# Filling work dealt out anew around the last routing, and expert weights fetched in two halves, in an attention and mixture-of-experts layer

## The chip, the cores and the metric

The kernel runs on one core of one Trainium2 chip. The metric is the device time in microseconds of one execution, as the median of several runs. All arithmetic is in 32-bit floats. The engines are called TensorE (PE), VectorE (DVE), ScalarE (ACT), GpSimd (POOL) and SyncE (SP). SP computes nothing: it reads numbers into registers, waits on semaphores and issues DMA transfers, in the order of its own instruction stream.

## The reference

The input is 8 sequences of 512 tokens with 512 features. The layer is attention followed by a mixture of experts, each with a layer norm before it, a layer norm behind it and a residual:

```
x = x + layernorm(attention(layernorm(x)))      # 16 heads, latent keys and queries, softmax
x = x + layernorm(moe(layernorm(x)))

moe(t) = routed(t) + shared(t)
shared(t) = relu(t @ shared_up)**2 @ shared_down           # 512 -> 1024 -> 512
scores = sigmoid(t @ router.T)                             # 16 experts, in 4 groups
chosen = the best 2 experts within the best 2 groups       # ranked by scores + e_bias
w = scores[chosen] / sum(scores[chosen])
routed(t) = sum over e in chosen of  w[e] * relu(t @ w_up[e])**2 @ w_down[e]    # 512 -> 256 -> 512
```

## The kernel before, in words

**Stages.** The attention stage works through the 8 sequences, each in 16 steps (4 groups of 4 heads, by 4 tiles of 128 queries). A step issues the score matmuls, softmax, transposes and weighted sums of its own. Work of the sequence before (output projection, norms, routing) and of the next one (projections) is put at fixed steps by `beside`. Every routed token row is scattered by GpSimd into a table in DRAM, sorted by expert (`send`, L780). When the last sequence is routed, `plan` counts the tiles of each expert and makes `lists`: for each place a first row in the table, an expert, and a flag that says whether the expert differs from that of the place three before. Then comes the routed stage over 79 tiles of 128 gathered rows, and then a tail, in which the shared expert of the last three half sequences is computed and all results are summed, normed and stored.

**The order of PE.** PE's instructions run in the order in which the program traces them. The other engines are ordered by a scheduler; in the routed stage and in the tail, SP's order is the program's too.

**Filling work.** The shared expert is computed in half sequences, numbered k = 0 to 15. Each consists of eight up chunks (L817; cost 1.72 in the planner's unit, microseconds: 8 matmuls as the trace counts them, a relu on ScalarE at L825, a square at L827 on VectorE or at L829 on ScalarE) and four down pieces (L836, cost 3.43). The halves 0 to 12 wait in the list `waiting`, and `fill(room)` takes pieces from its front while room is left. In the last sequence (`last_sequence`), fills stand between the output projection, the transposes of the normed rows, the router's logits and `assign`. `assign` turns the chosen experts into table rows through two small matmuls (ps_pos, L755 and L756), and `plan` needs one more (ps_plan, L908). What is left in `waiting` is emptied after the plan by `fill(1e9)`. The squares of halves 13 to 15 (`LATE = 3`) are on ScalarE, the others on VectorE.

**The routed stage.** There are three sets of weight tiles (`NBUF = 3`; `set_up` and `set_down`, 512 KB each), and places that are neighbours in time use different sets. In turn n, PE transposes the rows of place n+1 (pt_g, L966; the copy is at L968), computes the up product of place n (hg, L983) and the down product of place n-1 (yg, L998). VectorE scales the result, and GpSimd adds it into a sum in DRAM by scattered rows (L1007). SP fetches ahead, at the end of the turn:

```
            if n + AHEAD < NTILES:
                fetch_rows(places[n + AHEAD])          # AHEAD = 3
            if n + NBUF - 1 < NTILES:
                fetch_weights(places[n + NBUF - 1])    # place n + 2
```

`fetch_rows` reads one list entry into a register (L948) and issues one transfer (L950). `fetch_weights` reads two entries, the expert and the flag (L953, L954), and issues two conditional transfers, up (L956) and down (L959); where the flag is 0, nothing is moved. The weights of place n+2 go into the set that place n-1 has used, so the up transfer waits until `up(n-1)` is done and the down transfer until `down(n-1)` is done. The weight tiles also take memory that the tiles of the attention stage held, so that the first fetch waits for the scatters out of `ao`.

Of the kernel before, what the change touches and what calls it, by code (L numbers as in the profile page):

```python
# [18 lines left out]
P = 128  # L19
# [20 lines left out]
def sandwich_kernel(  # L40
# [28 lines left out]
    nc = tc.nc  # L69

    B, S, D = x.shape
# [26 lines left out]
    NTILES = (TOP_K * T) // P + NE - 1  # L98
    NBUF = 3
    THIRD = -(-NTILES // NBUF)  # L100
    NPLACES = NBUF * THIRD
    places = [j for j in range(NPLACES) if j % NBUF * THIRD + j // NBUF < NTILES]
# [157 lines left out]
    def normalize(dst, src, rstd, off, i):  # L260
        nc.scalar.activation(
            dst, src, AF.Identity, bias=off[:, i : i + 1], scale=rstd[:, i : i + 1]
        )
# [310 lines left out]
    def last_sequence(prev, fill):  # L574


        b = B - 1
        xT[b] = sh.tile([P, NK, S], F32, tag="xnT", name=f"xT_{b}")
        pt_den = ps_o.tile([P, NT, P], F32, tag="o", name=f"pt_d_{b}_last")
        ps_ctx = ps_o.tile([P, S], F32, tag="o", name=f"o_{b}_last")  # L580
        acc = [None] * NT

        def most(i):
            acc[i] = ps_o.tile([P, D], F32, tag="o", name=f"ps_acc_{i}")
            nc.tensor.matmul(acc[i], lhsT=ones[0:1, :], rhs=bo[0:1, :], start=True, stop=False)
            for c in range(NK - 1):
                out_of_group(acc[i], b, c, i)

        denominators(b, NGRP - 1)
        for i in range(2):  # L590
            most(i)
        keys_first(*prev, range(4))
        turn_denominators(b, NGRP - 1, pt_den)
        weighted_sum(b, NGRP - 1, ps_ctx)
        for i in range(NT):
            if i > 1:
                most(i)
            out_of_group(acc[i], b, NK - 1, i)
        fetch_x()
        for i in range(NT):  # L600
            ps, row, xb = acc[i], ao[:, i, 0:D], res[b][:, i, :]
            normalize(row, ps, *norm_stats([ps], f"o{b}_{i}"), 0)
            nc.vector.tensor_tensor(xb, xb, row, ALU.add)
            normalize(row, xb, *norm_stats([xb], f"f{b}_{i}"), 0)
        fill(3.4)
        for i in range(NT):
            turn_rows(ao, xT[b], i, f"f{b}")
            if i > 0:
                logits(b, i - 1)
            if i < NT - 1:  # L610
                fill(1.7)
        logits(b, NT - 1)
        sigmoid(b)
        groups(b)
        experts(b)
        fill(5.1)
        assign(b)
        weights(b)
        for i in range(NT):
            send(b, i)  # L620
# [190 lines left out]
    def shared_up_chunk(b, a, i):  # L811

        if i == 0:
            hT[b] = sh.tile([P, NH, HALF], F32, tag="hT", name=f"hT_{b}_{a}")
        ps = ps_o.tile([P, S], F32, tag="o", name=f"h_{b}_{a}_{i}")
        for k in range(NK):
            nc.tensor.matmul(  # L817
                ps[:, 0:HALF],
                lhsT=wsu[:, k, i * P : (i + 1) * P],
                rhs=xT[b][:, k, a * HALF : (a + 1) * HALF],  # L820
                start=(k == 0),
                stop=(k == NK - 1),
            )
        h = hT[b][:, i, :]
        nc.scalar.activation(h, ps[:, 0:HALF], AF.Relu)  # L825
        if 2 * b + a < 2 * B - LATE:
            nc.vector.tensor_tensor(h, h, h, ALU.mult)  # L827
        else:
            nc.scalar.square(h, h)  # L829
# [107 lines left out]
    def routed(rt, lists, expert):  # L937

        xg, xgT, hg, share, to = {}, {}, {}, {}, {}
        sets = []  # L940
        for i in range(NBUF):
            sets.append((
                rt.tile([P, NK, INTER], F32, name=f"set_up_{i}"),
                rt.tile([P, NI, D], F32, name=f"set_down_{i}"),
            ))

        def fetch_rows(j):
            row = nc.sync.value_load(lists[0:1, 0, j : j + 1], min_val=0, max_val=NE * REGION)  # L948
            xg[j] = rt.tile([P, W], F32, tag="xg", name=f"xg_{j}", bufs=4)
            nc.sync.dma_start(xg[j], table[bass.ds(row, P), :])  # L950

        def fetch_weights(j):
            e = nc.sync.value_load(lists[0:1, 1, j : j + 1], min_val=0, max_val=NE - 1)  # L953
            load = nc.sync.value_load(lists[0:1, 2, j : j + 1], min_val=0, max_val=1)  # L954
            wu, wd = sets[j % NBUF]
            nc.sync.dma_start(  # L956
                wu, w_up[bass.ds(e, 1)].rearrange("o (c p) i -> p (o c) i", p=P), cond=load
            )
            nc.sync.dma_start(  # L959
                wd, w_down[bass.ds(e, 1)].rearrange("o (c p) d -> p (o c) d", p=P), cond=load  # L960
            )

        def turn(j):
            pt = ps_o.tile([P, NK, P], F32, tag="o", name=f"pt_g_{j}")
            for k in range(NK):
                nc.tensor.transpose(pt[:, k, :], xg[j][:, k * P : (k + 1) * P], ident)  # L966
            xgT[j] = rt.tile([P, NK, P], F32, tag="xgT", name=f"xgT_{j}", bufs=4)
            nc.scalar.copy(xgT[j], pt)  # L968

            each = rt.tile([P, NE], F32, tag="each", name=f"each_{j}", bufs=2)  # L970
            share[j] = rt.tile([P, 1], F32, tag="share", name=f"share_{j}", bufs=4)
            nc.vector.scalar_tensor_tensor(
                each, experts_, expert[:, j : j + 1], xg[j][:, D:NUMBER],
                ALU.is_equal, ALU.mult, accum_out=share[j],
            )
            to[j] = rt.tile([P, 1], I32, tag="to", name=f"to_{j}", bufs=6)
            nc.vector.tensor_copy(to[j], xg[j][:, NUMBER : NUMBER + 1])

        def up(j):
            ph = ps_o.tile([P, S], F32, tag="o", name=f"hg_{j}")  # L980
            for i in range(NI):
                for k in range(NK):
                    nc.tensor.matmul(  # L983
                        ph[:, i * P : (i + 1) * P],
                        lhsT=sets[j % NBUF][0][:, k, i * P : (i + 1) * P],
                        rhs=xgT[j][:, k, :],
                        start=(k == 0),
                        stop=(k == NK - 1),
                    )
            h = rt.tile([P, NI * P], F32, tag="hgT", name=f"hgT_{j}", bufs=4)  # L990
            nc.scalar.activation(h, ph[:, 0 : NI * P], AF.Relu)  # L991
            nc.vector.tensor_tensor(h, h, h, ALU.mult)  # L992
            hg[j] = h

        def down(j, n):
            py = ps_o.tile([P, D], F32, tag="o", name=f"yg_{j}")
            for i in range(NI):
                nc.tensor.matmul(  # L998
                    py,
                    lhsT=hg[j][:, i * P : (i + 1) * P],  # L1000
                    rhs=sets[j % NBUF][1][:, i, :],
                    start=(i == 0),
                    stop=(i == NI - 1),
                )
            y = rt.tile([P, D], F32, tag="y", name=f"y_{j}", bufs=4)
            nc.vector.tensor_scalar(y, py, share[j], None, ALU.mult)  # L1006
            nc.gpsimd.indirect_dma_start(  # L1007
                out=sums[n % 2][:, :],
                out_offset=bass.IndirectOffsetOnAxis(ap=to[j], axis=0),
                in_=y,  # L1010
                in_offset=None,
                compute_op=ALU.add,
            )

        AHEAD = 3
        for n in range(NBUF - 1):
            fetch_weights(places[n])
        for n in range(AHEAD):
            fetch_rows(places[n])
        turn(places[0])  # L1020
        for n in range(NTILES + 1):
            if n + 1 < NTILES:
                turn(places[n + 1])
            if n < NTILES:
                up(places[n])
            if n > 0:
                down(places[n - 1], n - 1)
            if n + AHEAD < NTILES:
                fetch_rows(places[n + AHEAD])
            if n + NBUF - 1 < NTILES:  # L1030
                fetch_weights(places[n + NBUF - 1])

# [53 lines left out]
    LATE = 3  # L1088
# [65 lines left out]
    with tc.manual_schedule(engines={mybir.EngineType.PE}):  # L1154
# [8 lines left out]
        def fill(room):  # L1163
            while waiting and room > 0:
                cost, f, _ = waiting.pop(0)
                f()
                room -= cost
# [47 lines left out]
        while waiting[0][0] == UP:  # L1215
            waiting.pop(0)[1]()
        last_sequence(prev, fill)
        lists, expert = plan()
        fill(1e9)
    until_routed.close()  # L1220
# [3 lines left out]
    for k in range(2 * B - LATE, 2 * B):  # L1224
# [4 lines left out]
        for n, (cost, f) in enumerate(shared_list(k, one)):  # L1229
            items.append((f, 2 * k if n == NH + 3 else None))  # L1230
            if len(items) > 6 and n % 2 == 1:
                c = next(early, None)
# [12 lines left out]
    with tc.manual_schedule(engines={mybir.EngineType.PE, mybir.EngineType.SP}):  # L1245
        n = 0
# [48 lines left out]
```

## Time and profile before

| | |
|---|---|
| three runs | 1643.39 us median, 1639.08 to 1643.61 |
| profiled execution | 1646.31 us, of which the span of instructions is 1644.6 us |
| PE busy | 1563.2 us (95% of the span) |
| VectorE, ScalarE, GpSimd busy | 1003.3, 843.5 and 208.0 us |
| mean granted clock of PE | 0.975 |
| routed stage | first rows turned at 1225.8 us, last scatter issued at 1550.4 us |

The profile is of one execution on the chip. Times in it are microseconds from the first instruction. PE is the matmul stream and PEld the loads of stationary operands beside it. PEclk is the share of full speed at which PE's clock was granted. A row of a timeline gives start, duration, engine, line, operation, `out<-in`, the number of instructions that are merged in it, and in brackets the idle time before it and what ended it. A row of a line's instructions gives the count, then the shortest, median and longest duration in ns, then the first and last start. A row of SP's waits gives who waited for whom, the microseconds in total, the times and the longest. SP's instructions are not counted as busy time on the page. A row by windows gives the busy time of PE, PEld, DVE, ACT and POOL with the number of instructions, then PE's clock, the mean busy share of the 16 DMA engines and the GB/s that they moved.

### The profile page before, as it was taken

The page shows a single profiled execution, that of the slowest core. Times are in us where ns is not written, and L with a number is a line of the kernel's source. Part 1 is how long each engine was busy: PE and PEld are TensorE (multiplying, and loading weights), DVE is VectorE, ACT ScalarE, POOL GpSimd, SP SyncE. Part 2 cuts the span into 40 slices and gives each one's busy share as a digit, 9 for nine tenths or more (in the row PEclk, how much of TensorE's full clock was granted, in tenths as well). Part 3 has the DMA queues.
Part 4 walks back from the last instruction along what each step waited for, and adds up shares of the span by engine and source line. Part 5 has one row for each costly group of instructions (what it writes and reads, how often), then busy time and mean ns, then how long its engine had stood idle before and what let it go on. Part 6 is the DMA issues. An engine that isn't in the chain of part 4 may idle for free.

```text
span 1644.6 us, 25313 instructions
## 1 busy us (share of the span) xinstructions
PE 1563.2 (95%) x8010; PEld 916.2 (56%) x8010; DVE 1003.3 (61%) x2942; ACT 843.5 (51%) x1998; POOL 208.0 (13%) x193
## 2 busy tenths in 40 slices
PE   6999799999999999999999999999989999899996
PEld 3554454555455545555544545456557777677754
DVE  4667874776587577758766866774433333333298
ACT  5876665575466557556655755654312222122245
POOL 0000011002000100200010020011014333333300
PEclk8999899999999999999999999999989999999998
DMA  4016666567566655755564565552457778997695
GB/s 130 1 36 198 186 201 199 145 192 246 158 182 187 214 165 167 219 154 153 154 200 125 150 210 149 166 149 87 165 178 133 141 138 191 310 244 154 134 366 200
DMA packets 170022, 282.89 MB, mean 172 GB/s; under 512 B 21152, under 2 KB 86688, under 8 KB 169632
## 3 DMA queue, kind: packets, MB, share of 16 engines
q1 hardware_dynamic: 153392, 242.72, 48.2%
q0 software_dynamic: 16496, 38.54, 11.8%
q8 instruction: 64, 1.05, 0.3%
q14 instruction: 70, 0.57, 0.1%
HBM read 224.43 MB, written 132.92 MB: 217 GB/s over the span
## 4 chain that ended last, share of the span: by engine, by line
PE 67%; DVE 15%; DMA 7%; ACT 7%; SPq 2%; issue 2%; DVEq 0%; POOL 0%; POOLq 0%; ACTq 0%
PE y L836 9%; PE hg L983 7%; PE yg L998 7%; PE h L817 6%; PE pt L454 6%; PE ps_ao L623 6%; PE s L387 5%; PE o L521 4%; DMA set_up<-in_L_ffn_w_up_dram 2%; DMA turned<-pB 2%; DVE pB L473 2%; ACT pb L417 2%; PE ps_v L347 2%; PE pt_g L966 2%; PE ps_k L360 1%
## 5 line engine op out<-in xcount | busy, mean ns | idle before, releaser
L417 ACT ACTIVATE pb<-pb,nmax 128x512 f32<-128x512 f32 x256 | 182.7, 715 | 191.1 <-DVE nmax L405 184.1
L817 PE MATMUL h<-xT,wsu 128*128 128x256 f32 x1024 | 240.7, 391 | 0.6 <-ACT hT L825 0.6
L836 PE MATMUL y<-wsd,hT 128*128 128x512 f32 x512 | 231.6, 603 | 0.0
L405 DVE CUSTOM_DVE_ANT_0 pb<-s,rope 128x512 f32<-128x512 f32 x256 | 166.7, 685 | 97.5 <-PE s L387 97.0
L817 PEld LDWEIGHTS h<-xT,wsu 128*128 128x128 f32 x1024 | 198.1, 196 | 48.8 <-issue 10.2
L417 ACT ACTIVATE p<-p,nmax 128x512 f32<-128x512 f32 x256 | 181.5, 710 | 29.9 <-DVE nmax L405 29.5
L405 DVE CUSTOM_DVE_ANT_0 p<-s,rope 128x512 f32<-128x512 f32 x256 | 167.6, 684 | 27.1 <-PE s L387 26.4
L454 PEld LDWEIGHTS pt<-ident,p 128*128 128x128 f32 x1024 | 111.6, 142 | 99.7 <-issue 22.7
L473 DVE STREAM_TRANSPOSE pB<-pb 128x1024 f32<-128x1024 f32 x108 | 133.8, 1238 | 49.8 <-DMA turned<-pB 36.7
L983 PE MATMUL hg<-xgT,set_up 128*128 128x128 f32 x1264 | 155.1, 276 | 8.2 <-DMA set_up<-in_L_ffn_w_up_dram 7.1
L836 PEld LDWEIGHTS y<-wsd,hT 128*128 128x128 f32 x512 | 97.0, 193 | 116.2 <-issue 108.6
L387 PE MATMUL s<-k,q 32*128 32x512 f32 x1024 | 156.7, 647 | 0.0
L454 PE MATMUL pt<-ident,p 128*128 128x128 f32 x1024 | 142.2, 281 | 12.7 <-DVE ctx L528 12.6
L983 PEld LDWEIGHTS hg<-xgT,set_up 128*128 128x128 f32 x1264 | 147.4, 192 | 11.4 <-issue 5.8
L1007 POOL DMA_INDIRECT sums<-y,to x79 | 122.6, 1552 | 222.4 <-DVE y L1006 190.1
L998 PE MATMUL yg<-set_down,hgT 128*128 128x512 f32 x316 | 148.5, 593 | 0.0
L495 POOL COPY wide<-rden 128x512 f32<-128x512 f32 x32 | 19.6, 613 | 977.3 <-PE ps_ao L623 233.7
L992 DVE TENSOR_TENSOR hgT<-hgT 128x256 f32<-128x256 f32 x79 | 33.6, 426 | 156.4 <-ACT hgT L991 156.4
L521 PE MATMUL o<-pTb,v 128*32 128x512 f32 x496 | 114.5, 604 | 7.8 <-DMA pTb<-turned 7.8
L968 ACT COPY xgT<-pt_g 128x512 f32<-128x512 f32 x79 | 46.2, 586 | 139.4 <-PE pt_g L966 139.4
L521 PE MATMUL o<-pT,v 128*32 128x512 f32 x496 | 116.5, 604 | 0.2 <-DVE pT L464 0.2
L623 PE MATMUL ps_ao<-wo,ctx 128*128 128x512 f32 x224 | 98.5, 593 | 0.0
(233 smaller groups left out, 2073.2 us busy)
## 6 DMA issues: line engine op xcount, KB each, us to landing
turned<-pB SPq DMA_DIRECT2D x432, 128.0 KB
pTb<-turned SPq DMA_DIRECT2D x108, 512.0 KB
set_up<-in_L_ffn_w_up_dram SPq DMA_DIRECT2D x79, 512.0 KB
set_down<-in_L_ffn_w_down_dram SPq DMA_DIRECT2D x79, 512.0 KB
xg<-table SPq DMA_DIRECT2D x79, 272.0 KB
end<-sums SPq DMA_DIRECT2D x32, 512.0 KB
sums<-table SPq DMA_DIRECT2D x40, 256.0 KB
x<-in_L_attn_x_dram SPq DMA_DIRECT2D x32, 256.0 KB
```

Source lines behind the costliest of these rows:

```text
L387: nc.tensor.matmul(tiles[h], lhsT=q[r0 : r0 + HEAD_DIM, qt * P : (qt + 1) * P], rhs=k[r0 : r0 + HEAD_DIM, :], start=True, stop=True,)
L405: last_max[b, g] = nc.vector.tensor_tensor_reduce(out=p_h, in0=tiles[h], in1=rope[b, qt], scale=-1.0, scalar=3.0e38, op0=ALU.add, op1=ALU.min,
L417: nc.scalar.activation(p_h, p_h, AF.Exp, bias=nmax[:, h : h + 1], scale=-1.0, accum_out=dens[b, m][:, qt, h : h + 1],)
L454: nc.tensor.transpose(pt[:, c, :], pr[:, c * P : (c + 1) * P], ident)
L473: turn = nc.vector.transpose(pB[:, :, hs].rearrange("p j h c q -> p (h c) j q"), pb[:, hs].rearrange("p h (c j q) -> p (h c) j q", j=NB, q ...
L521: nc.tensor.matmul(to if h < NP else to.rearrange("p (n q) -> p n q", q=BLK), lhsT=vs[b][:, c, col : col + HEAD_DIM], rhs=pT[:, h, c, :] i ...
L623: nc.tensor.matmul(ps, lhsT=ctxs[b, c][:, i * P : (i + 1) * P], rhs=wo[:, c, :], start=(c == 0 and b < B - 1), stop=(c == NK - 1),)
L817: nc.tensor.matmul(ps[:, 0:HALF], lhsT=wsu[:, k, i * P : (i + 1) * P], rhs=xT[b][:, k, a * HALF : (a + 1) * HALF], start=(k == 0), stop=(k ...
L836: nc.tensor.matmul(ysum[c], lhsT=hT[b][:, i, t * P : (t + 1) * P], rhs=wsd[:, i, :], start=(i == 0), stop=(i == NH - 1),)
L983: nc.tensor.matmul(ph[:, i * P : (i + 1) * P], lhsT=sets[j % NBUF][0][:, k, i * P : (i + 1) * P], rhs=xgT[j][:, k, :], start=(k == 0), sto ...
L998: nc.tensor.matmul(py, lhsT=hg[j][:, i * P : (i + 1) * P], rhs=sets[j % NBUF][1][:, i, :], start=(i == 0), stop=(i == NI - 1),)
L1007: nc.gpsimd.indirect_dma_start(out=sums[n % 2][:, :], out_offset=bass.IndirectOffsetOnAxis(ap=to[j], axis=0), in_=y, in_offset=None, compu ...
```

## The change

There are three edits. In `last_sequence`, the fill ahead of `assign` grows from 5.1 to 6.8, and a new `fill(5.0)` stands between `last_sequence` and `plan`. The squares of half 12 move from VectorE to ScalarE. In the routed stage, `fetch_weights` fetches one part, up or down, and is called once for each: at the end of turn n the down weights of place n+2 and then the up weights of place n+3. Ahead of the first turn, three up parts and two down parts are fetched instead of two of each. Each call reads both list entries.

```
-        fill(5.1)
+        fill(6.8)
         assign(b)
...
-        if 2 * b + a < 2 * B - LATE:
+        if 2 * b + a < 2 * B - LATE - 1:
             nc.vector.tensor_tensor(h, h, h, ALU.mult)
         else:
             nc.scalar.square(h, h)
...
-        def fetch_weights(j):
+        def fetch_weights(j, part):
             e = nc.sync.value_load(lists[0:1, 1, j : j + 1], min_val=0, max_val=NE - 1)
             load = nc.sync.value_load(lists[0:1, 2, j : j + 1], min_val=0, max_val=1)
-            wu, wd = sets[j % NBUF]
             nc.sync.dma_start(
-                wu, w_up[bass.ds(e, 1)].rearrange("o (c p) i -> p (o c) i", p=P), cond=load
-            )
-            nc.sync.dma_start(
-                wd, w_down[bass.ds(e, 1)].rearrange("o (c p) d -> p (o c) d", p=P), cond=load
+                sets[j % NBUF][part],
+                (w_up, w_down)[part][bass.ds(e, 1)].rearrange("o (c p) n -> p (o c) n", p=P),
+                cond=load,
             )
...
-        for n in range(NBUF - 1):
-            fetch_weights(places[n])
+        for n in range(NBUF):
+            fetch_weights(places[n], 0)
+            if n < NBUF - 1:
+                fetch_weights(places[n], 1)
...
             if n + NBUF - 1 < NTILES:
-                fetch_weights(places[n + NBUF - 1])
+                fetch_weights(places[n + NBUF - 1], 1)
+            if n + NBUF < NTILES:
+                fetch_weights(places[n + NBUF], 0)
...
         last_sequence(prev, fill)
+        fill(5.0)
         lists, expert = plan()
         fill(1e9)
```

## The prediction

> **What bounds the kernel now.** I read the page's shares first (TensorE, PE, is busy 95% of the span), then the timeline of PE where the last sequence is routed, then the table by windows, and then, because the change issues more on SyncE, SP's waits, its instructions by line and its timeline. The timeline of PE around the last routing:
>
> ```profile
> 1186.15 5.43 PE L817 MATMUL h<-xT,wsu 128*128 128x256 f32 x24
> 1194.29 0.42 PE L755 MATMUL ps_pos<-cum,ones 128*128 128x80 f32 x2 [2.71 <-DVE total L737]
> ...
> 1199.70 1.62 PE L908 MATMUL ps_plan<-spread,ones 128*128 128x384 f32 x2 [4.78 <-DVE spread L906]
> 1201.11 11.11 PE L817 MATMUL h<-xT,wsu 128*128 128x256 f32 x40
> 1212.06 13.90 PE L836 MATMUL y<-wsd,hT 128*128 128x512 f32 x32
> 1225.79 1.04 PE L966 MATMUL pt_g<-ident,xg 128*128 128x128 f32 x8
> ```
>
> Three up chunks (24 matmuls) fill 5.4 us; then PE idles 2.71 and 4.78 us for VectorE, 7.5 us in all. After the plan come five up chunks and four down pieces, and the first gathered tile is turned at 1225.8. The windows (PE, PEld, DVE, ACT, POOL busy, then clock, DMA share, GB/s):
>
> ```profile
> 1186.00:1201.30 15.30, 7.81 (x34) 6.16 (x34) 11.55 (x70) 1.37 (x4) 3.31 (x4) 0.81 0.13 47
> 1201.30:1226.00 24.70, 24.70 (x75) 15.24 (x74) 5.35 (x25) 2.50 (x6) 4.46 (x5) 0.91 0.71 249
> 1250.00:1380.00 130.00, 130.00 (x794) 96.84 (x793) 46.10 (x165) 31.88 (x67) 51.17 (x33) 1.00 0.76 139
> 1380.00:1480.00 100.00, 92.39 (x545) 66.70 (x544) 31.91 (x114) 21.84 (x46) 35.65 (x23) 1.00 1.00 274
> ```
>
> PE never idles in 1250 to 1380, where no expert changes, and loses 7.6 us in 1380 to 1480, where most tiles bring a new expert and the DMA engines are always busy. SP's largest wait in this stage (us in all, times, longest), and its list reads by line:
>
> ```profile
> SPq L959 <- PE yg L998: 58.8, 71, 3.5
> ```
>
> ```profile
> L953 SPq TENSOR_LOAD <-lists x79: 263/268/957, 1202.3 to 1535.5; - x79
> L953 SPq FUSED_REGOPS  x79: 147/153/187, 1203.2 to 1536.5; - x79
> L953 SPq SEQ_ASSERT  x79: 18/18/32, 1203.4 to 1536.7; - x79
> ...
> L954 SPq TENSOR_LOAD <-lists x79: 261/271/763, 1203.5 to 1536.8; - x79
> ```
>
> SP's timeline over one tile without new weights:
>
> ```profile
> 1301.11 0.34 SPq L950 DMA_DIRECT2D xg<-table  x1
> 1302.89 0.07 SPq L956 DMA_DIRECT2D set_up<-in_L_ffn_w_up_dram  x1
> 1304.15 0.07 SPq L959 DMA_DIRECT2D set_down<-in_L_ffn_w_down_dram  x1
> 1305.06 0.34 SPq L950 DMA_DIRECT2D xg<-table  x1
> ```
>
> These lines decide. SP is not counted as busy on the page, yet it works most of a tile's 3.95 us (1301.11 to 1305.06): its one wait, for the place of the down weights, is 58.8 us in 71 waits, 0.83 us a tile. So its own work is about 3.1 us a tile. Most of it is reading list entries into registers: each is a TENSOR_LOAD, a FUSED_REGOPS and a SEQ_ASSERT.
>
> **The change, part by part.**
>
> *1. Filling work.* A program-order count of the queue of filling pieces gives four down pieces spent in the fills before, and `fill(5.1)` takes three up chunks of 1.72; `fill(6.8)` takes four. The new `fill(5.0)` takes the next three before the plan's matmul, so that one up chunk and four down pieces are left behind it. No matmul is added. Four chunks at 1.73 us (5.18 for three in the chain of waits) end at 1193.1; three more take 5.2 us beside VectorE's chain from ps_pos (1194.9) to spread (1199.6), 4.6 us long. Both gaps close but for some 0.3 us: 7.2 us.
>
> The clock comes on top. In the rows, it is below 1 in the two windows above: the five chunks behind the gap took 10.9 us by the chain of waits, not 5 x 1.73 = 8.65, and the plan's two matmuls 1.62. From the trace's clock records, half clock ran from 1195.5 to 1205.8; PE worked 6.1 us of it, so lost 3.05 us. The Trainium skill ("TensorE: Matmul & The Clock Gate", Part 1, "What's actually happening") puts the clock at half after one idle window of about 3.4 us, until one such window is busy: that would cost 1.7 us. I use the trace's 3.05, since the first gap also belongs to it. PE would then reach the first gathered tile at 1225.8 - 7.2 - 3.0 = 1215.6.
>
> *2. Squares.* All eight squares of the last filled half move from VectorE (426 ns each) to ScalarE (414 ns at L829). Three of the former stand inside VectorE's routing chain (1188.7, 1191.2, 1193.2), 0.33 us each in the chain of waits: slots, scatters and plan come 1.0 us earlier. ScalarE is idle 1.3 us between these relus and 12.8 us after the third (1192.0 to 1204.8), and its exponential for the routing is issued before them: cost 0. Without that cover, 8 x 0.41 = 3.3 us.
>
> *3. Start of the routed stage.* SP's first weight fetch went out at 1208.96, when the last scatter from ao had landed; now 1207.9. To the first rows SP took 4.5 us (1213.43). It now issues five fetches instead of four, each with its own pair of list reads: three pairs more at 1.14 us (from 1301.50, the load of L953, to 1302.63, the start of L956) and one issue of 0.68 us, 4.1 us. First rows: 1216.6; readable some 3.2 us later, as the fourth tile's were before (1216.8 to 1220.0): about 1220. So PE waits 4.4 us there and starts 5.8 us earlier, not 10. A new spell of half clock costs 0 to 1.7 us; step 5 hides it.
>
> *4. What the up weights gain.* They are now asked for a tile earlier, when PE is through with up(n), and have two tiles before use, not one. Landing took 6 to 8 us in the crowded stretch (the chain has 6.95, 7.95, 8.03), against 7.9 for two tiles. By the starts of L983, the stretch loses 11.1 us against 3.94 a tile. At most those 11.1 us are won. Part is bandwidth, though: seven tiles in a row took 4.7 us each with the DMA share at 1.0, and the bytes stay; on SP's transfer queue the rows of a tile stand behind one up and one down set as before.
>
> *5. What the split costs on SP.* Each tile now reads two list entries more. No matching wait is removed. Nothing is added in waiting: down(n-1), which the down fetch awaits, stands behind up(n) in PE's order, so the up fetch behind it finds its place free. Queued behind it are the rows of the next tile, and PE's pt_g waits for those. Work per tile, as the period less its wait in the trace, has a median of 3.12 and a mean of 3.20 us without new weights (55 tiles), and a mean of 3.85 with (15). The pair: median 1.14, mean 1.17. So 4.27 to 4.37 without and 4.9 to 5.0 with. Both exceed PE's 3.945 and the second also DMA's 4.7: SP sets the pace of the whole stage. The Trainium skill has a dearer price ("DMA: Bandwidth & Descriptors", "Latency and other measured facts": a floor of some 600 ns for a tensor_load), against 268 and 271 ns in 79 rows each. By it the two loads would add 0.66 us more a tile, 50 us in all. These rows are the operation itself, so I take them.
>
> *The sum.* Rows of the fourth tile go out at 1216.6 + 3 x 1.14 = 1220.0, plus up to 0.8 for two stores of the shared result that stand among these fetches: 1220.5. From there to the rows of tile 79 are 75 tiles, 15 with weights: 60 x 4.27 + 15 x 4.9 = 330 with medians, 60 x 4.37 + 15 x 5.0 = 337 with means. I take 334: some of the slow loads in the means may be chance, but a hiccup of 0.3 us every 128 SP instructions scales with their number. Hence 1554.5. Behind it come 3.1 us for landing, 0.44 for the turn, two ups at 1.79 and three downs at 1.72: 12.3, so 1566.8. Before, the last down ended at 1549.2. The tail hangs on the last scatter either way and moves by all of it: +17.6 us. PE is ahead of its rows by some 2.7 us at the start and loses 0.35 a tile, so it is caught after about eight tiles; steps 1 and 4 and the clock are then swallowed. Span 1644.6 + 17.6 = 1662; its own time 1646.3 + 17.6 = 1663.9. That execution stands 2.9 us above the median of the three runs, so the median becomes 1661.0.
>
> **The rivals.**
> - *SP keeps up (faster).* If a list read cost less, or the second pair were not executed, SP would stay hidden. The place is SP's 0.83 us of slack a tile; below that price for the added pair PE sets the pace. The gain is then 5.8 us at the start plus up to 11.1: 1626, or, if bandwidth keeps most of the latter, 1634. For it: SP appears nowhere in the chain inside the stage. Against it: 1.14 is above 0.83, and every read in the trace is executed.
> - *The two cancel.* A pair at about 0.95 us gives SP a pace of 4.05 to 4.1: 330 - 75 x 0.19 = 316, so the stage ends at 1549, the time of before: about 1643. Only a misread price brings this.
> - *Dearer reads.* At the page's 600 ns: 1661 + 50 = 1711; at half that surcharge 1686. Slow loads (up to 957 ns) exist, but few.
> - *The edits do not do what they say.* If SP ran its queue in another order, the up fetch could stand ahead of rows that are due; SP's order is written out, so I give this little.
>
> **How the numbers follow.** SP sets the pace: 0.82, at 1661, own range 1654 to 1669 (medians to means, either count of the stores, a small wait more). Dearer: 0.08. Cancelled or nearly so, 1638 to 1654: 0.05, split over the same and slower. Faster: 0.05. The range 1650 to 1672 holds the first and the upper part of the third. A measurement of this kernel tells about 0.3% from no change, 5 us (1639 to 1643.6 in three runs): faster by more 0.05, within it 0.03, slower 0.92.
>
> **What would show it.** Right: reads of the list in SP's rows x158 each; SP's wait for yg falls from 58.8 us to a few; pt_g waits for xg by 0.3 to 0.5 us in most tiles (none now); tiles 4.2 to 4.4 us apart in quiet stretches at full clock; no wait for set_up; gaps before ps_pos and ps_plan below 1 us; first pt_g near 1220. Wrong: tiles still 3.95 us apart in 1250 to 1380, or SP waiting for yg by over 0.3 us a tile. If gaps on PE persist around the plan, step 1 is wrong, by at most the 5.8 us of step 3.

## The result: 4.3% slower, for the predicted reason, by about four times the predicted amount

| | before | changed |
|---|---|---|
| median of the runs shown together | 1641.46 us (1639.08 to 1643.61, 4 runs) | 1711.95 us (1707.93 to 1715.79, 4 runs) |
| ratio, 95% interval | | 1.043 [1.0397, 1.0462] |
| profiled execution, its span | 1646.3, 1644.6 us | 1710.1, 1708.4 us |
| PE busy | 95% of the span | 92% |

The forecast was 1661 us, 1650 to 1672. The change cost 70.5 us by the medians and 63.8 us by the spans of the two profiled executions, where the sum had 17.6. The timeline of PE around the last routing, changed kernel:

```profile
1184.55 7.15 PE L817 MATMUL h<-xT,wsu 128*128 128x256 f32 x32
1191.97 0.42 PE L755 MATMUL ps_pos<-cum,ones 128*128 128x80 f32 x2 [0.27 <-DVE total L737]
...
1192.44 5.40 PE L817 MATMUL h<-xT,wsu 128*128 128x256 f32 x24
1197.67 0.81 PE L908 MATMUL ps_plan<-spread,ones 128*128 128x384 f32 x2
1198.32 1.89 PE L817 MATMUL h<-xT,wsu 128*128 128x256 f32 x8
1200.05 13.90 PE L836 MATMUL y<-wsd,hT 128*128 128x512 f32 x32
1221.70 1.94 PE L964 MATMUL pt_g<-ident,xg 128*128 128x128 f32 x8 [7.76 <-DMA xg<-table]
```

The gaps of 2.71 and 4.78 us are 0.27 and nothing, and the plan's two matmuls take 0.81 instead of 1.62 us. PE is through with its filling work at about 1213.9, and then waits 7.76 us for the first gathered rows. The same stretches as before in windows (the second now ends at 1222, where the first rows were turned):

```profile
1186.00:1201.30 15.30, 15.03 (x68) 12.26 (x67) 11.69 (x73) 6.40 (x16) 5.02 (x6) 1.00 0.19 74
1201.30:1222.00 20.70, 12.94 (x32) 5.65 (x31) 0.30 (x3) 1.17 (x2) 2.73 (x3) 0.91 0.70 236
1250.00:1380.00 130.00, 110.79 (x645) 78.36 (x646) 38.12 (x134) 25.95 (x54) 41.69 (x27) 0.99 0.57 113
1380.00:1480.00 100.00, 80.63 (x460) 56.57 (x458) 28.56 (x97) 18.63 (x39) 30.20 (x21) 0.98 0.85 217
```

In 1250 to 1380, where PE never idled, it now does 110.79 us of work in 130. DMA engines are less busy than before too (0.57 against 0.76; 0.85 against 1.00 in the next row), so the loss is not for want of bandwidth. PE's waits from 1186 to 1600 (us in all, times, longest), and SP's for a place for weights (1222 to 1600; for the down weights these were 58.8 us in 71 waits before):

```profile
PE pt_g L964 <- DMA xg<-table: 63.5, 44, 7.8
PE hg L981 <- DMA set_up<-in_L_ffn_w_up_dram: 5.2, 1, 5.2
```

```profile
SPq L955 <- PE hg L981: 2.9, 5, 1.3
...
SPq L955 <- PE yg L996: 1.2, 2, 0.8
```

PE waits for rows, and SP hardly waits for anybody: SP sets the pace. Its reads of the list by line:

```profile
L953 SPq TENSOR_LOAD <-lists x158: 262/270/1041, 1199.6 to 1598.9; - x158
L954 SPq TENSOR_LOAD <-lists x158: 260/269/1046, 1200.5 to 1599.5; - x158
```

There are 158 of each, as foreseen, with the medians of before. But a tile without new weights takes SP 4.9 us (mean of 53), not 4.3. One such tile on SP, then the reads of line 954 in 1242 to 1250, then GpSimd in the same place:

```profile
1242.86 0.34 SPq L950 DMA_DIRECT2D xg<-table  x1
1244.71 0.07 SPq L955 DMA_DIRECT2D set_down<-in_L_ffn_w_down_dram  x1
1246.97 0.07 SPq L955 DMA_DIRECT2D set_up<-in_L_ffn_w_up_dram  x1
1247.89 0.34 SPq L950 DMA_DIRECT2D xg<-table  x1
```

```profile
L954 SPq TENSOR_LOAD <-lists x3: 272/273/993, 1243.8 to 1248.9; - x3
```

```profile
1243.15 1.55 POOL L1005 DMA_INDIRECT sums<-y,to  x1 [2.39 <-DVE to L975]
1247.09 1.55 POOL L1005 DMA_INDIRECT sums<-y,to  x1 [2.39 <-DVE to L975]
```

From down fetch to up fetch SP takes 2.26 us with nothing to wait for, and one of the three reads lasted 993 ns instead of 273. By its own record it began at 1245.41, 2.26 us after GpSimd had begun to issue a scatter into the sums. Such a read occurs in 70 of 75 tiles. In the following table, SP's instructions between the rows of the fourth tile and those of tile 79 (75 tiles) are taken from the trace one by one; a read is slow where more than 0.38 us pass until the next instruction, and its excess is what goes beyond 0.318 us. A wait is what passes beyond 0.065 us between SP's last register move and the transfer of weights. The experiments are in the table already.

| kernel | SP, 75 tiles | reads | slow | their excess | waits for a weight place |
|---|---|---|---|---|---|
| before | 316.3 us | 225 | 16 | 4.1 us | 58.0 us |
| changed | 374.1 us | 375 | 82 | 34.3 us | 2.7 us |
| e1, changed, one pair of reads | 315.7 us | 225 | 7 | 1.7 us | 63.1 us |
| e2, before, two pairs of reads | 375.3 us | 375 | 84 | 32.3 us | 3.4 us |
| e4, changed, other partition | 372.3 us | 375 | 77 | 31.6 us | 3.0 us |
| e5, changed, no scatter | 340.9 us | 375 | 3 | 0.9 us | 2.7 us |
| e10, changed, storing scatter | 364.8 us | 375 | 73 | 21.8 us | 4.0 us |

### The profile page after: what moved, and what is told of

It reads as the page before. It is cut to its first block, busy times and chain, and to the rows that moved or that the text cites. A ratio compares the mean times of both kernels' runs of the same rounds, so it can differ in the third digit from the quotient of the medians.

```text
span 1708.4 us, 25783 instructions
## 1 busy us (share of the span) xinstructions
PE 1574.0 (92%) x8010; PEld 916.1 (54%) x8010; DVE 1002.3 (59%) x2934; ACT 846.4 (50%) x2006; POOL 207.6 (12%) x193
## 5 line engine op out<-in xcount | busy, mean ns | idle before, releaser
L981 PE MATMUL hg<-xgT,set_up 128*128 128x128 f32 x1264 | 159.4, 281 | 5.2 <-DMA set_up<-in_L_ffn_w_up_dram 5.2
L981 PEld LDWEIGHTS hg<-xgT,set_up 128*128 128x128 f32 x1264 | 152.5, 197 | 6.2 <-issue 5.9
L454 PE MATMUL pt<-ident,p 128*128 128x128 f32 x1024 | 142.5, 281 | 12.3 <-DVE ctx L528 12.1
L964 PE MATMUL pt_g<-ident,xg 128*128 128x128 f32 x316 | 50.1, 283 | 63.8 <-DMA xg<-table 63.5
```

Of the source, the lines that this page charges most:

```text
L454: nc.tensor.transpose(pt[:, c, :], pr[:, c * P : (c + 1) * P], ident)
L981: nc.tensor.matmul(ph[:, i * P : (i + 1) * P], lhsT=sets[j % NBUF][0][:, k, i * P : (i + 1) * P], rhs=xgT[j][:, k, :], start=(k == 0), sto ...
```

## The experiments

Medians and ratios are against the kernel before, run on the same chip: 1644.42 us (40 runs) for e1 to e4, 1644.91 us (56 runs) for e5 to e8, 1645.80 us (13 runs) for e9 to e11.

### e1 and e2: the second pair of reads, taken away and put in alone

e1 is the changed kernel, with the expert and the flag read once, at the up fetch, and the registers kept for the down fetch:

```diff
+        read = {}
         def fetch_weights(j, part):
-            e = nc.sync.value_load(lists[0:1, 1, j : j + 1], min_val=0, max_val=NE - 1)
-            load = nc.sync.value_load(lists[0:1, 2, j : j + 1], min_val=0, max_val=1)
+            if j not in read:
+                read[j] = ( ...the same two loads... )
+            e, load = read[j]
```

> The changed kernel, but the expert and flag of a place are read into registers once, at the up fetch, and kept for the down fetch one turn later: two list reads fewer per tile. SP theory (SP's list reads set the pace): SP's own work falls to about 3.1 us a tile, PE sets the pace again at 3.95 us a tile, the wait of SP for yg returns to some 0.8 us a tile, reads that are slow are hidden in it; the first pt_g comes some 2 us earlier (1219.5), the stage takes 312 to 323 us: 1628 to 1640 us. Rival (the new order of the fetches, up ahead of the next rows, is what costs): 1700 us or more, as the order is kept.

e2 is the kernel before, with the same two reads executed once more between the two transfers:

```diff
             nc.sync.dma_start( wu, ... cond=load )
+            e = nc.sync.value_load(lists[0:1, 1, j : j + 1], min_val=0, max_val=NE - 1)
+            load = nc.sync.value_load(lists[0:1, 2, j : j + 1], min_val=0, max_val=1)
             nc.sync.dma_start( wd, ... cond=load )
```

> The kernel before, but with expert and flag read a second time between the up and the down fetch of a place: the reads of the change without its order, its fill or its squares. SP theory: tiles 4.7 to 5.0 us apart, PE waits for xg, stage 50 to 70 us longer: 1690 to 1715 us. Rival (the order costs): 1641 to 1645, as before.

Measured: e1 1649.56 us (17 runs), ratio 1.0027 [1.0008, 1.0046]; e2 1708.41 us (4 runs), 1.0374 [1.0343, 1.0406]. SP's wait for the place of the down weights in e1 and then in e2, and the waits of PE in e1, from 1226 on:

```profile
SPq L961 <- PE yg L1002: 61.0, 72, 2.6
```

```profile
SPq L961 <- PE yg L1000: 2.5, 2, 1.5
```

```profile
PE pt_g L970 <- DMA xg<-table: 12.5, 13, 2.0
PE hg L987 <- DMA set_up<-in_L_ffn_w_up_dram: 1.3, 1, 1.3
```

So the second pair is nearly the whole loss, and it needs no other part of the change: e2 is within 4 us of the changed kernel, and e1 within 0.5% of the kernel before. Without the pair, SP's slack is back (61.0 us against 58.8). But e1 is not faster than before: it missed its own forecast (1628 to 1640), and that of the rival of an SP that keeps up (1626 to 1634). What ate that gain is taken up at e3 and e6.

### e3 and e11: the filling work, with and without the squares

e3 is the kernel before, with the fills and the squares of the change and its old fetching. e11 is e3 with the squares left on VectorE.

```diff
-        fill(5.1)
+        fill(6.8)
...
-        if 2 * b + a < 2 * B - LATE:          # e11 keeps this line
+        if 2 * b + a < 2 * B - LATE - 1:
...
         last_sequence(prev, fill)
+        fill(5.0)
```

> The kernel before with the new fills and the squares on ScalarE alone. SP theory: the gaps before ps_pos and ps_plan close, no half clock there, PE is ready for the first tile near 1214 and waits for its rows until 1217 to 1218: 8 us less, so about 1634 us. Rival (whatever is gained at the fill is lost in waiting for rows, weights or scatters): within 2 us of 1642.

> The kernel before with the new fills, but the squares of half 12 left on VectorE. Step 2 has it that three squares in VectorE's routing chain cost 1.0 us: the last scatter starts 19.7 to 20 us after the sigmoid as before, instead of 19.0, and the fourth up chunk no longer ends just before ps_pos but waits some 1.3 us for VectorE; first turn near 32.5 instead of 31.4 us. If the squares cost nothing there, 19.0 and 31.4. The time differs by 1 us, below what a round tells.

Measured: e3 1640.14 us (22 runs), 0.9973 [0.9959, 0.9988]; e11 1641.40 us (4 runs), 0.9969 [0.9942, 0.9995]. The two can't be told apart by their times. In the timeline of PE in e11 small gaps are left:

```profile
1192.35 0.42 PE L755 MATMUL ps_pos<-cum,ones 128*128 128x80 f32 x2 [0.97 <-DVE total L737]
...
1198.67 0.88 PE L908 MATMUL ps_plan<-spread,ones 128*128 128x384 f32 x2 [0.46 <-DVE spread L906]
```

They add up to 1.43 us, against 0.27 in the changed kernel. All starts can be counted from the end of the last sigmoid's exponential on ScalarE (L686), which lies ahead of every edit:

| us after that | plan's matmuls begin | filling work done | first rows asked for | first gathered tile turned | stage of 79 tiles lasts |
|---|---|---|---|---|---|
| before | 13.4 | 39.6 | 27.1 | 39.4 | 323.4 |
| changed | 12.9 | 29.2 | 33.0 | 37.0 | 390.8 |
| e1 | 12.9 | 29.2 | 29.7 | 34.6 | 331.4 |
| e3 | 12.9 | 29.2 | 27.8 | 31.4 | 323.5 |
| e11 | 14.3 | 30.6 | 29.0 | 33.1 | 325.2 |
| e6 | 12.9 | 29.2 | 29.6 | 34.7 | 325.1 |
| e7 | 12.9 | 29.2 | 21.9 | 29.0 | 329.0 |
| e8 | 12.9 | 29.2 | 21.9 | 29.0 | 324.4 |
| e9 | 12.9 | 29.2 | 23.2 | 29.0 | 321.4 |

The filling work moves PE 10.4 us forward (39.6 to 29.2). In e3, 8.0 of it arrive at the first tile; in the changed kernel 2.4, since rows are asked for later. By its trace, e3 is 7.7 us shorter than before from there to the last instruction. By the medians it is 4.3 us, about half of what was expected (1634 us).

### e4, e5 and e10: what makes a read slow

Three theories: reads are held up at the partition that they read from; they are held up by the scatter into the sums; or the slow ones only follow from there being more reads. e4 reads the same values from partition 64. e5 leaves out the scatter of the routed results into the sums. e10 has a scatter that stores and doesn't add. So the output of both lacks routed results.

```diff
-            e = nc.sync.value_load(lists[0:1, 1, j : j + 1], ...)      # e4: likewise for row and flag
+            e = nc.sync.value_load(lists[64:65, 1, j : j + 1], ...)
...
-            nc.gpsimd.indirect_dma_start(out=sums[n % 2][:, :], ...)   # e5: whole call
...
-                compute_op=ALU.add,                                    # e10: this line
```

> The changed kernel, with SP reading the lists from partition 64 instead of partition 0 (the lists are the same on all partitions). Slow reads: 79 of 374 take 0.35 to 1.04 us instead of 0.27, 34 us in all, and they are those that start 2.0 to 3.0 us after a scatter of GpSimd. If it is the low partitions that are busy then, the reads are fast again and the time falls by about 30 us, to 1680. If a read is held up wherever it goes, the count of slow reads and the time stay (1708 to 1715).

> The changed kernel without the scatter of the routed results into the sums (the routed part is left out of the output). If the slow list reads come from the scatter, they vanish (34 us of excess to under 5), a tile takes SP some 4.3 to 4.4 us instead of 4.95, and the time falls by about 30 us to 1675 to 1685; the down product still waits for nothing new. If they come from the rows that land or from SP itself, 70 or more slow reads stay and the time stays above 1700.

> The changed kernel with the scatter of the routed results storing instead of adding (the sums then hold only the last result of each row). If it is the adding (reading the sums back, adding, writing) that holds up SP's list reads, the slow reads fall from 82 to a few and the time to about 1680. If it is the scatter as such[...], 70 or more slow reads stay, and 1705 to 1715 us.

Measured: e4 1709.20 us (4 runs), 1.0383 [1.0351, 1.0414]; e5 1675.05 us (2 runs), 1.019 [1.0145, 1.0235]; e10 1705.09 us (2 runs), 1.0355 [1.0325, 1.0386]. The reads of the two lines in e5:

```profile
L953 SPq TENSOR_LOAD <-lists x158: 262/268/483, 1201.9 to 1567.7; - x158
L954 SPq TENSOR_LOAD <-lists x158: 260/267/1011, 1202.7 to 1568.3; - x158
```

e4 changes nothing: of the two partitions read, neither is better. In e5, with as many reads, 3 of 375 are slow instead of 82. SP's time for 75 tiles falls by 33.1 us, as much as the excess of the slow reads (34.3 to 0.9), and the loss against the kernel before falls from 4.3 to 1.9%. So the scatter makes reads slow, and this is the part of SP's loss that the prediction missed. Even then e5 stays slower than before (1.019): the added reads at 0.27 us each suffice to make SP the bound.

The place of a slow read against the scatter ahead of it says when. In the changed kernel, of 72 reads in the stage that began 2.0 to 3.0 us after GpSimd's scatter began, 69 were slow (above 350 ns); of 78 that began 1.0 to 1.9 us after, none. The scatter's lines on the two pages, changed kernel and e10 (mean ns behind the comma):

```profile
L1005 POOL DMA_INDIRECT sums<-y,to x79 | 122.6, 1552 | 288.2 <-DVE to L975 159.9
```

```profile
L1005 POOL DMA_INDIRECT sums<-y,to x79 | 76.0, 962 | 325.2 <-DVE to L975 240.9
```

In e10, where the scatter takes GpSimd 0.96 us instead of 1.55, the slow reads begin earlier (four in five of them 1.36 to 2.11 us after) and are shorter (mean 0.57 us against 0.69). In both they begin some 0.4 us after GpSimd's own instruction has ended. So with adding the hold-up is longer and later, but the scatter as such is enough.

In the kernel before, only 2 of 220 reads began 2.0 to 3.0 us after a scatter, and both were slow. Its down fetch waited for yg at just that time, and SP's next read mostly followed at 3.0 to 3.1 us (51 reads, 7 of them slow). **The wait sheltered the reads.** That is why the rows of before priced them too low.

What of the scatter holds up a read stays open. It is not simply the amount of data under way: by the trace's DMA records of the changed kernel, the scatter's packets move from 2.0 us after its start on, and most densely 3.25 to 4.25 us after it (54 of the 126 packets of a scatter, on average). Of the 72 reads that began in that time only 2 were slow.

### e6 to e9: why one pair of reads didn't make it faster, and a version that is

e1 lost in two places that e3 did not. It starts the first tile 3.2 us later (34.6 against 31.4), and it loses more in the crowded tiles. The following is what each trace loses against 3.945 us a tile (by the starts of the up products). In the column of the first tile, 2.3 us are no loss: the first turn has no down product, so that the first two steps last 2.3 us longer than one tile even where nothing waits.

| us lost | first tile | tiles 1 to 37 | 38 to 62 (crowded) | 63 on |
|---|---|---|---|---|
| before | 2.3 | -0.1 | 11.1 | -0.5 |
| changed | 3.1 | 29.7 | 30.4 | 16.7 |
| e1 | 3.6 | 0.0 | 15.0 | 1.4 |
| e3 | 2.3 | -0.1 | 11.3 | -0.5 |
| e6 | 3.9 | -0.1 | 8.8 | 1.2 |
| e7 | 4.0 | -0.1 | 13.2 | -0.5 |
| e8 | 4.0 | -0.1 | 7.7 | -0.5 |
| e9 | 2.7 | -0.1 | 6.8 | -0.5 |

e6 is e1 with rows asked for one turn earlier, to test whether the rows stand behind weights that are due later:

```diff
-            xg[j] = rt.tile([P, W], F32, tag="xg", name=f"xg_{j}", bufs=4)
+            xg[j] = rt.tile([P, W], F32, tag="xg", name=f"xg_{j}", bufs=5)
...
-        AHEAD = 3
+        AHEAD = 4
```

> Reads once per place, and the rows fetched four places ahead instead of three (five buffers). In the run with reads once, the waits of PE for set_up had gone and 12.5 us of waits for xg had come: the rows of a place stand behind 1 MB of weights that are due later. If that order is the cause, the waits for xg go and the stage falls from 331 to 316 to 322 us: 1634 to 1640. If the crowded stretch is bound by DMA throughput, the 11 to 15 us lost there stay, whatever waits for what: stage 325 to 331, 1644 to 1650.

e7 is e3 with rows ahead of weights at the start of the stage:

```diff
+        fetch_rows(places[0])
         for n in range(NBUF - 1):
+            fetch_rows(places[n + 1])
             fetch_weights(places[n])
-        for n in range(AHEAD):
-            fetch_rows(places[n])
```

> The kernel before with the new fills and squares, and ahead of the first turn the rows of two places fetched before the first weights. PE stood ready 29.2 us after the sigmoid and had its rows at 31.4: 2 us less than with the fills alone, 1638 against 1640. If the weights are then late instead, the same as with the fills alone.

e8 puts e6 and this start together. It also fetches the last two places, whose weight sets are out of turn because one place is left out, one turn later:

```diff
+        fetch_rows(places[0])
         for n in range(NBUF):
+            fetch_rows(places[n + 1])
             fetch_weights(places[n], 0)
...
+        def in_turn(m):
+            return places[m] % NBUF == m % NBUF
...
-            if n + NBUF - 1 < NTILES:
-                fetch_weights(places[n + NBUF - 1], 1)
-            if n + NBUF < NTILES:
-                fetch_weights(places[n + NBUF], 0)
+            for part, late in ((1, 2), (0, 3)):
+                for m in (n + late, n + late - 1):
+                    if m < NTILES and m >= NBUF - part and in_turn(m) == (m == n + late):
+                        fetch_weights(places[m], part)
```

> Fills, squares, up and down fetched apart with the list read once per place, rows four places ahead, rows first ahead of the first turn, and at the end the two places whose set is used out of turn fetched after the last use of it. If rows and weights are only late by order: head 8 us shorter and 2 more from the rows, stage 315 to 320: 1625 to 1633, below both kernels. If DMA throughput binds the crowded stretch: 1636 to 1640.

e9 is e8 with the very first up weights ahead of the very first rows:

```diff
-        fetch_rows(places[0])
         for n in range(NBUF):
-            fetch_rows(places[n + 1])
             fetch_weights(places[n], 0)
+            if n == 0:
+                fetch_rows(places[0])
+            fetch_rows(places[n + 1])
```

> As the version with everything put together (reads once, rows four places ahead, rows first), but the up weights of the first place go out ahead of the first rows. There PE turned the first tile at 29.0 us after the sigmoid, then waited for its up weights some 3 us and fell to half clock for 3.4 us (first two up products 7.9 us apart instead of 3.9 plus the 2.3 of the first turn). If only the order at the start is in the way, the first up product starts near 30 us and 2 to 4 us are won: 1635 to 1637. If the transfers there are bound by throughput, the wait moves back to the rows: 1638 to 1640.

Measured: e6 1641.87 us (22 runs), 0.9978 [0.9963, 0.9993]; e7 1638.46 us (22 runs), 0.9962 [0.9947, 0.9976]; e8 1639.21 us (19 runs), 0.9962 [0.9945, 0.9979]; e9 1638.24 us (6 runs), 0.995 [0.9931, 0.9969].

e6 takes the crowded loss from 15.0 to 8.8 us, so that much of it was a matter of order in e1; its time lies between its two forecasts (1634 to 1640, and 1644 to 1650). PE waits for rows only once, for the very first ones, where e1 had 12.5 us in 13 waits behind these. Weights are waited for again, as before:

```profile
PE hg L987 <- DMA set_up<-in_L_ffn_w_up_dram: 6.8, 8, 1.5
PE pt_g L970 <- DMA xg<-table: 5.5, 1, 5.5
```

e7 turns the first tile as soon as the filling work is done (29.0 against 31.4 in e3), but its stage is 5.5 us longer than that of e3. The timelines of PE and of ScalarE in e7, where the first up product should begin:

```profile
1213.90 3.13 PE L983 MATMUL hg<-xgT,set_up 128*128 128x128 f32 x16 [2.21 <-ACT xgT L968]
```

```profile
1212.78 0.59 ACT L848 COPY ysh<-y 128x512 f32<-128x512 f32 x1 [8.21 <-DMA sums<-ysh]
1213.26 1.08 ACT L968 COPY xgT<-pt_g 128x512 f32<-128x512 f32 x2
```

On ScalarE, the copy of the turned rows stands behind a copy of the shared result, and that one waits for a store, which SP issues at 1207.67 behind the first weights. So the rows are early, and the next thing in line is late. The up product then runs at half clock (3.13 us), and 13.2 us are lost in the crowded tiles where e3 loses 11.3.

e8 was to add these gains up, but at 1639.21 us it missed the forecast for lateness by order alone (1625 to 1633). e9 has the same wait at its first up product as e7, without the half clock. The timeline of PE there, and its window of the crowded stretch, in which PE does 95.05 us of work against 92.39 before, with the DMA engines as busy:

```profile
1222.87 2.05 PE L987 MATMUL hg<-xgT,set_up 128*128 128x128 f32 x16 [2.30 <-ACT xgT L972]
```

```profile
1380.00:1480.00 100.00, 95.05 (x568) 69.53 (x567) 34.87 (x119) 22.84 (x48) 37.35 (x24) 1.00 1.01 284
```

From the sigmoid to the last instruction, the trace of e9 is 11.8 us shorter than that of before (446.5 against 458.3). By the runs it is 7.6 us: e9 beats both kernels, by 0.5% [0.3, 0.7] against the one before. It missed its better forecast, too (1635 to 1637); the 2.3 us behind the shared result's store are left in it. Of the crowded loss, 6.8 us are left, with the DMA engines always busy; whether these are bandwidth was not tested. e7, e8 and e9 are too close to be ordered by their medians.

## Why the prediction was right or wrong, point by point

**Right: SP becomes the bound, and the sign.** The decision point was a price of 0.83 us for the added pair. e1 and e2 put the pair away and in alone, and show it to be above that point: 316 us of SP for 75 tiles with 58 to 63 us of waits, against 374 to 375 us with about 3.

**Step 1, filling work: right.** Predicted were 7.2 us of gaps and 3.05 of clock, 10.2 in all; measured are 10.4 (9.0 in e11, without the squares). The clock is 1.00 in the first window, 0.81 before. With the estimate of 1.7 us from the Trainium skill ("TensorE: Matmul & The Clock Gate", Part 1, "What's actually happening") for the clock, the sum would have been 8.9, further from the measurement than with the trace's 3.05. That does not speak against the page's rule: the 10.2 us of half clock in the trace of before are three of its windows of about 3.4 us, and the estimate had counted one.

**Step 2, squares: right.** 1.0 us predicted; the filling work of e11 ends 1.4 us later than that of e3 (30.6 and 29.2), and the plan's matmuls begin 1.4 us later. Nothing of it can be seen in the medians.

**Step 3, the start: right in kind, too small.** The first weight fetch went out at 1206.62 and the first rows at 1217.72, 11.1 us later, where the step had 8.7. Two stores of the shared result stand among these fetches and hold up the queue by some 1.6 us, one of them by waiting; the step had put them behind the first rows, at 0.8 us. One slow read of 1046 ns makes up the rest. SP's queue there (L849 are the stores):

```profile
1210.40 0.38 SPq L955 DMA_DIRECT2D set_up<-in_L_ffn_w_up_dram  x1
1210.88 0.44 SPq L849 DMA_DIRECT2D sums<-ysh  x1
1213.58 0.38 SPq L955 DMA_DIRECT2D set_down<-in_L_ffn_w_down_dram  x1
1215.45 0.38 SPq L955 DMA_DIRECT2D set_up<-in_L_ffn_w_up_dram  x1
1216.57 0.34 SPq L849 DMA_DIRECT2D sums<-ysh  x1
1217.72 3.97 SPq L950 DMA_DIRECT2D xg<-table  x4
```

So PE waited 7.76 us, not 4.4, and the first tile gained 2.4 us, not 5.8. The start of SP's pace was nearly met all the same (1221.4 against 1220.5), but by luck: this execution came to its last routing 1.6 us earlier.

**Step 4, what the up weights gain: it was not there.** "At most those 11.1 us" held, but e1 shows that the order of the change gains none of it: 15.0 us are lost there. The waits for up weights went, but for one of 1.3 us in e1, and 12.5 us of waits for rows came. In the kernel before they were, from 1226 to 1550:

```profile
PE hg L983 <- DMA set_up<-in_L_ffn_w_up_dram: 7.1, 11, 1.4
```

An up set that is asked for a tile earlier stands in front of rows that are due sooner. The prediction said that rows stood behind one up and one down set "as before", and gave that no price. e6, with rows one turn earlier, gets 2.3 of the 11.1 us. (The seven tiles in a row that the step has at 4.7 us each lasted 4.9 on average, six of them 4.7 to 5.6.)

**Step 5 and the sum: the failed step is the price of a read.** The step had 1.14 to 1.17 us for the added pair; by SP's work less its waits in the two traces it was 1.5 us a tile, of which 0.4 are slow reads. It is this term that sank the number:

| term | predicted | measured | difference |
|---|---|---|---|
| rows of the fourth tile | 1220.5 | 1221.4 | +0.9 us |
| 75 tiles on SP, without slow reads and waits | 334 | 337.1 | +3.1 us |
| slow reads | in it | 34.3 | +34.3 us |
| SP's waits for places | 0 | 2.7 | +2.7 us |
| last rows to the last down product | 12.3 | 17.1 | +4.8 us |
| tail | as before | 95.8 | +0.4 us |

The differences add up to 46.2 us, which is 63.8 less 17.6. Without slow reads the step was right: in e5 a tile without new weights takes SP 4.30 us in the median and 4.39 in the mean, where it had 4.27 to 4.37. The step took "these rows are the operation itself" as its reason, and those rows were of reads that a wait kept away from the scatter. It noted slow loads of up to 957 ns and left it open whether they were chance, without asking what else was going on when they occurred. The change removed the wait that sheltered them.

From the last rows to the last down product it took longer because of a wait of PE near the end of the stage, changed kernel:

```profile
1588.51 0.63 PE L964 MATMUL pt_g<-ident,xg 128*128 128x128 f32 x4 [0.88 <-DMA xg<-table]
1594.36 3.36 PE L981 MATMUL hg<-xgT,set_up 128*128 128x128 f32 x16 [5.23 <-DMA set_up<-in_L_ffn_w_up_dram]
```

One place is left out of the order, so the last two use weight sets out of turn. The up fetch for one of them, which moves nothing, stands in the program ahead of an up product that uses the same set, and that product waits for it. It then runs at half clock (3.36 us instead of 1.95). The prediction had "no wait for set_up". In e8 and e9 this fetch is a turn later, and the loss of 1.2 to 1.4 us in the last tiles of e6 and e1 is gone.

**The rivals.** *Dearer reads* came nearest in number: by the price that the Trainium skill states ("DMA: Bandwidth & Descriptors", "Latency and other measured facts"), 1711 us. Not for its reason: the median read took 0.27 us here, not 0.6, and what the sum missed comes from 82 reads that are longer by 0.42 us each. (With its two register instructions, FUSED_REGOPS and SEQ_ASSERT, one read takes 0.59 us in these traces.) As a floor, the price would also have made the kernel before SP-bound: three reads a tile at 0.33 us more are 0.99 us, above its slack of 0.83. *SP keeps up* fell, and so did its gain, by e1. *The two cancel* is out by 69 us. *The edits do not do what they say* did not come about, since SP's order is the written one; but this order itself puts an up set ahead of rows that are due sooner (step 4).

**The signs to look for.** Reads x158, SP's wait nearly gone, the gaps closed and pt_g near 1220 (1221.7): as predicted. Tiles at 4.2 to 4.4 us and waits for xg of 0.3 to 0.5 us: no, the waits were 1.4 us on average, in 44 tiles, and SP took 5.0 us a tile over all.

## What to carry to other kernels

An engine that only issues can be the bound without being busy in a profile: before adding to its stream, compare its work in a period with the wait it has left, and read a dynamic address once and keep it in its register. Durations taken from rows hold for the moment at which those rows ran; if the engine waits in each period, ask what passes during that wait, and look where the few slow rows lie against other engines' work before calling them chance. Asking for one transfer earlier makes another later in the same queue: put them in the order in which they are due (here rows before weights, but the very first weights before the very first rows).

## What the hardware showed that was not expected

- A read of a list entry into an SP register takes 0.27 us, but 0.70 us in the mean, and up to 1.04, where it begins 2 to 3 us after GpSimd has begun to issue a scatter that adds into DRAM (69 of 72 slow). Reading from partition 64 instead of 0 makes no difference (77 slow, against 82), and without the scatter 3 of 375 are slow. A few reads are slow before the first of these scatters, too (1046 ns at 1211.94); their cause is not known.
- A conditional transfer that moves nothing still takes its place in the queue and in the order of waits, but only 0.07 us of SP's time, against 0.38 for one that moves weights. Of a skipped fetch, nearly all the cost is in reading its operands.
- PE lost its clock again where it waited for the first rows: after 7.76 us of idling it ran at half clock for 6.8 us by the clock records, and the first eight transposes took 1.94 us instead of 1.04. The step's 0 to 1.7 us for this spell is about what these rows give, 0.9 there and 0.85 in the up product behind it (2.80 instead of 1.95).
